# New ranks for the convolution and preparation stages, delta-A weights on GpSimd, and five projection chunks in flight, in a selective-scan and attention kernel on one core

## The chip, the core and the metric

The kernel runs on one NeuronCore of a Trainium2 chip. Five engines work there side by side, each through its own instructions in a fixed order: TensorE (PE in the profile; its weight loads are PEld), VectorE (DVE), ScalarE (ACT), GpSimd (POOL) and SyncE (SP), which here issues all transfers. They wait for each other through semaphores. The metric is the device time of one execution in microseconds (us). The kernel before took 10973.58 us in the median of three runs (10972.01 to 10994.84).

## The reference, cut to what matters

Eight images of 96 channels and 64 x 64 pixels go through two layers. L is 4096 pixels, DI is 192 inner channels, K is 4 scan directions with 16 states each.

```python
# layer 0: x = x + conv_block(group_norm(x))
xh = layernorm(xh)                         # over the 96 channels
xi, z = split(xh @ in_proj_w.T + in_proj_b)   # 192 + 192 channels
xi = silu(depthwise_conv3x3(xi) + conv_b)
xs = stack([xi by rows, xi by columns] and both reversed)   # 4 directions
dts, Bs, Cs = split(xs @ x_proj_w)
delta = softplus(dts @ dt_proj_w + dt_proj_b)
A = -exp(A_log)
h[t] = exp(delta[t] * A) * h[t-1] + delta[t] * xs[t] * B[t];  y[t] = C[t] . h[t]
y = sum of the 4 directions, put back in place, + D * xs
out = (layernorm(y) * silu(z)) @ out_proj_w.T + out_proj_b
# layer 1: t = t + linear attention(layernorm(t)); t = t + quantised MLP(layernorm(t))
```

## The kernel before, in words

The images are taken in four pairs. For each pair there is a **scan** (line 586 on), some 1910 us long, in which DVE runs one scan instruction after the other. Between two scans lie two planned stages. In the first, `back` (line 825) turns the last pair's scan output into the input of the second layer while `project` (line 369) normalises and projects the new pair's images, in 16 chunks of 512 pixels. In the second, `tail` (line 963) runs the MLP of the last pair, in 16 chunks, while `convolve` (line 457) and `prepare` (line 503) make the scan's inputs for the new pair. Pair 0 has no `back` or `tail` beside it; after the last scan there is only `back` and then `tail`. Before the first `convolve`, `decay_weights` (line 282) makes the weights from which TensorE forms delta times A: from `A_log` it makes three bf16 parts, sends them to DRAM in 24 small transfers, reads them back spread over the partitions (`ac`), multiplies them with a mask into four tiles `awp` of 128 x 6144 bf16 (line 317) and writes these to DRAM (line 322), from where the scans load them.

**The planner.** Within a planned stage every instruction is first put down in a list (`P.add`) with its engine, a cost, what it reads and writes, the ring of buffers that it takes a buffer from, and a rank. `P.run` then emits them one by one with a clock of its own. On each engine it takes, among the instructions that could start within 0.1 us of the earliest one, that with the smallest rank:

```python
least = min(f[0] for f in found)
choices.append(min((f for f in found if f[0] <= least + 0.1), key=lambda f: (f[1], f[2])))
```

On the chip each engine then keeps to that order. An ACT instruction can name a set of tables (`"ln"`, `"silu"`, `"softplus"`); a table load is needed whenever the set changes.

**project.** A chunk is scaled with the group statistics (DVE, L423), normalised over channels by `norm` (PE L357, ACT square, PE L361, ACT Ln and Exp, DVE L365), scaled (DVE L428), and goes through three matmuls (L432, L438, L444), which ACT evacuates into the padded images and, with Silu, into `zt`, which is stored. The ring `chunk` of three empty slots allows three chunks in flight; PSUM has three banks `q` and two `hold`; there are eight `small` tiles when `back` is not beside it, and six when it is.

**convolve.** The 192 channels of both images lie in three tiles. Tiles 0 and 2 are convolved on DVE: for each image half h, 9 instructions of 128 x 2048 a tile (L473 and L476), which makes 36 a pair. Tile 1 goes through TensorE: 9 matmuls (L483) a chunk of 512 pixels, 72 a pair. Then ACT applies Silu to every chunk of `xi`. The ranks are -2 for half 0 and -1 for half 1, ahead of all that `prepare` and `tail` do.

**prepare.** For two pixel orders o, 8 chunks c, two directions k and three tiles T there is a unit of work, 96 a pair: TensorE makes the projections (L543, shared by three units, and L555), ACT the softplus `d` and its first bf16 part, DVE `du` = d * u (L560) and the remainder `rest` (L571), ACT the second part, POOL the third (L576); then 384 KB of `dp` and 256 KB of `du` go to DRAM for the scan. The rings are short: three `d`, `du` and `dp`, two `rest`, four PSUM banks `big`, which the convolution's matmuls also take. For o = 0 a unit of chunk c needs only chunk c of `xi`; for o = 1 POOL first copies the pixels in column order (`u`, L535, 24 a pair), which needs all chunks. The rank is (8 o + c) / 16.

**tail.** Its chunk i had rank i / 16, three chunks in flight; its norm needs the `"ln"` tables, the units of `prepare` need `"softplus"`.

`xi` is allocated where the tiles of `decay_weights` lay: tile 0 of `xi` and half of tile 1 overlap `awp`, so the first write of either waits until the last `awp` has been written to DRAM.

Of the kernel before, what the change touches and what calls it, by code (L numbers as in the profile page):

```python
# [14 lines left out]
AF = mybir.ActivationFunctionType  # L15
ALU = mybir.AluOpType
# [3 lines left out]
DIM = 96  # L20
# [6 lines left out]
F = 512  # L27
# [129 lines left out]
def vss_attn_ffn(ctx: ExitStack, tc: tile.TileContext, a: dict):  # L157
    nc = tc.nc
# [31 lines left out]
    convb = load("convb", [128, 2])  # L190
# [91 lines left out]
    def decay_weights():  # L282

        with tc.tile_pool(name="aprep", bufs=1) as wp:
            am = wp.tile([128, KD, 2, NS], F32, name="am")
            nc.sync.dma_start(am, a["alog"])
            nc.scalar.activation(am, am, AF.Exp)  # L290
            nc.vector.tensor_scalar(am, am, -1.0, None, ALU.mult)
            for i in range(3):
                ap = wp.tile([128, KD, 2, NS], BF16, name=f"ap{i}")
                nc.vector.tensor_copy(ap, am)
                if i < 2:
                    nc.vector.tensor_tensor(am, am, ap, ALU.subtract)
                for k in range(KD):
                    nc.sync.dma_start(ad[i, k, 0:128], ap[:, k, 0])
                    nc.sync.dma_start(ad[i, k, 128:DI], ap[0:64, k, 1])
            mask = wp.tile([128, 16], F32, name="mask")  # L300
            for p in range(3):
                nc.sync.dma_start(
                    mask[32 * p : 32 * p + 32],
                    ident[0:16, 0:16].unsqueeze(1).to_broadcast([16, 2, 16]),
                )
            for p in range(2):
                nc.sync.dma_start(mask[96 + 16 * p : 112 + 16 * p], ident[0:16, 0:16])
            for k in range(KD):
                ac = wp.tile([128, NE * NS], BF16, name="ac", bufs=2)
                for i, rows, n in ((0, slice(0, 96, 2), 6), (1, slice(1, 96, 2), 6), (2, slice(96, 128), 4)):  # L310
                    nc.sync.dma_start(
                        ac[rows],
                        ad[i, k].rearrange("(s c) n -> s (c n)", s=8).unsqueeze(0)
                        .to_broadcast([n, 8, NE * NS]),
                    )
                aw = wp.tile([128, 48, 16, 8], BF16, name="awp", bufs=2)
                nc.vector.tensor_tensor(
                    aw,
                    ac.rearrange("p (c n) -> p c n", n=8).unsqueeze(2).to_broadcast([128, 48, 16, 8]),
                    mask.unsqueeze(1).unsqueeze(3).to_broadcast([128, 48, 16, 8]), ALU.mult,  # L320
                )
                nc.sync.dma_start(awd[k], aw.rearrange("p c m n -> p (c m n)"))
# [43 lines left out]
            dst(), P["ncp" + n][:DIM], P["nrs" + n], ALU.mult, **kw),  # L366
            ("ncp" + n, "nrs" + n), written, new, rank)

    def project(P, pair, zs, ybuf, p1):

        pad = [t.rearrange("p (h w) -> p h w", w=HH + 2) for t in ybuf]
        for T in range(3):
# [6 lines left out]
        dma(P, 0.03, lambda: swap[:, 64:128], lambda: a["winT"][:, 128:DI], (), ("swap#1",), rank=-1)  # L379
        ring(P, p1, "xt", 2, [DIM, L])  # L380
        ring(P, p1, "zt", 2, [128, 2, F])
        P.ring("chunk", [None] * 3)
        stat = [[p1.tile([DIM, w], F32, name=f"{n}{b}") for n, w in (
            ("mv", 2), ("gm", 1), ("gd", 1), ("gv", 1), ("gr", 1))] for b in range(2)]
        bst = [p1.tile([DIM, NCH, 6], F32, name=f"bst{b}") for b in range(2)]
# [71 lines left out]
    def convolve(P, xi, ybuf, p1):  # L457

        pad = [t.rearrange("p (h w) -> p h w", w=HH + 2) for t in ybuf]
        diag = p1.tile([128, 9, 128], F32, name="diag")  # L460
        for t in range(9):
            dve(P, 0.28, lambda t=t: nc.vector.tensor_scalar(
                diag[:, t, :], ident, convw[:, 0, t : t + 1], None, ALU.mult), (), (f"diag#{t}",), (), -2)
        for h in range(2):
            for T in (0, 2):
                for t in range(9):
                    dy, dx = divmod(t, 3)
                    w = convw[:, half(T), t : t + 1]
                    v = pad[T][:, 32 * h + dy : 32 * h + dy + HH // 2, dx : dx + HH]
                    o = xi[T].rearrange("p (h w) -> p h w", w=HH)[:, 32 * h : 32 * h + HH // 2]  # L470
                    wr = [f"xi{T}#{c}" for c in range(4 * h, 4 * h + 4)]
                    if t == 0:
                        dve(P, 1.4, lambda o=o, v=v, w=w: nc.vector.tensor_scalar(  # L473
                            o, v, w, None, ALU.mult), (), wr, (), -2 + h)
                    else:
                        dve(P, 2.34, lambda o=o, v=v, w=w: nc.vector.scalar_tensor_tensor(  # L476
                            o, v, w, o, ALU.mult, ALU.add), (), wr, (), -2 + h)
            for c in range(4 * h, 4 * h + 4):
                r0 = c * ROWS
                n = f"pc.{c}"  # L480
                for t in range(9):
                    dy, dx = divmod(t, 3)
                    mm(P, 0.87, lambda n=n, t=t, r0=r0, dy=dy, dx=dx: nc.tensor.matmul(  # L483
                        P[n], diag[:, t, :], pad[1][:, r0 + dy : r0 + dy + ROWS, dx : dx + HH],
                        start=(t == 0), stop=(t == 8)), (f"diag#{t}",), (n,), ((n, "big"),), -2 + h)
                act(P, lambda c=c: xi[1][:, bass.ts(c, F)], lambda n=n: P[n], AF.Identity, 0.68, (n,),
                    (f"xi1#{c}",), (), -2 + h, bias=convb[:, 0:1])
        for c in range(NCH):
            for T in range(3):
                b_ = 0.0 if T == 1 else convb[:, half(T) : half(T) + 1]  # L490
                act(P, lambda T=T, c=c: xi[T][:, bass.ts(c, F)], lambda T=T, c=c: xi[T][:, bass.ts(c, F)],
                    AF.Silu, 0.72, (), (f"xi{T}#{c}",), (), -1 + c / 10, "silu", bias=b_)

    def spread(P, size, dst, T, src, reads, writes, rank):

# [467 lines left out]
    def tail(P, pair, t1, tn, tmp):  # L963
# [11 lines left out]
        for i in range(2 * NCH):  # L975
            c, b = divmod(i, 2)
            cs = bass.ts(c, F)
            rank = i / 16
            n = f"t.{i}"
            tf, xa, pa, t2, tq, hq, p2, y16, ot = (  # L980
                v + n for v in ("tf", "xa", "pa", "t2", "tq", "hq", "p2", "y16", "ot"))
# [42 lines left out]
    for pair in range(npair + 1):  # L1024

        new = {}
        if pair < npair:
            for name, shape, dtype in (
                ("zs", [2, DI, L], F32), ("us", [2 * DI, L], F32),
                ("dl", [KD, NT * TC // WC, 3, 16, NE, WC], BF16), ("du", [KD, NT, 16, NE, TC], F32),  # L1030
                ("bs", [KD, NT // NB, 2 * NS, NB * TC], F32),
                ("cs", [KD, NT // NB, 2 * NS, NB * TC], F32), ("ys", [KD, 16, L, NE], F32),
                ("t1", [2, DIM, L], F32), ("tn", [2, DIM, L], F32),
            ):
                new[name] = dram.tile(shape, dtype, name=name)
        with ExitStack() as pads, ExitStack() as xis:
            if new:

                yp = pads.enter_context(tc.tile_pool(name="yp", bufs=1, side="right"))
                ybuf = [yp.tile([128, (HH + 2) ** 2], F32, name=f"y{T}") for T in range(3)]  # L1040
            with ExitStack() as st:
                st.enter_context(tc.manual_schedule())
                P = Plan()
                tmp = st.enter_context(tc.tile_pool(name="bk", bufs=1))
                psum = banks(P, st, q=3, hold=2, **({"py": 2} if old else {}))
                ring(P, tmp, "small", 6 if old else 8, [DIM, F])
                if old:
                    back(P, pair - 1, old["ys"], old["us"], old["zs"], old["t1"], old["tn"], tmp, psum)
                if new:
                    project(P, pair, new["zs"], ybuf,  # L1050
                            st.enter_context(tc.tile_pool(name="p1", bufs=1, side="right")))
                P.run(table)
            if pair == 0:
                decay_weights()
            if new:
                xp = xis.enter_context(tc.tile_pool(name="xip", bufs=1))
                xi = [xp.tile([128, L], F32, name=f"xi{T}") for T in range(3)]
            with ExitStack() as st:
                st.enter_context(tc.manual_schedule())
                P = Plan()  # L1060
                tmp = st.enter_context(tc.tile_pool(name="tt", bufs=1))
                banks(P, st, **({"q": 3, "hold": 1} if old else {}), **({"big": 4} if new else {}))
                if old:
                    ring(P, tmp, "small", 4, [DIM, F])
                    tail(P, pair - 1, old["t1"], old["tn"], tmp)
                if new:
                    convolve(P, xi, ybuf, tmp)
                    prepare(P, tmp, xi, new["us"], new["dl"], new["du"], new["bs"], new["cs"])
                P.run(table)
        if new:  # L1070
            scan(new["dl"], new["du"], new["bs"], new["cs"], new["ys"])
        old = new
# [114 lines left out]
```

## Time and profile before

| | |
|---|---|
| median of three runs | 10973.58 us (10972.01 to 10994.84) |
| the profiled execution's own time | 10968.08 us |
| its span, from the first to the last instruction | 10966.3 us, granted TensorE clock 0.836 |
| busy: PE, DVE, ACT, POOL | 7884.5, 9068.7, 6970.9, 8003.3 us |
| first `project`, alone | 34 to 185 us |
| `decay_weights` after it | to 229 us |
| `convolve` and `prepare` of pair 0 | 229 to 613 us |
| the other three second stages (`tail`, `convolve`, `prepare`) | 2841 to 3316, 5538 to 6008, 8225 to 8699 us |
| the last `tail`, alone | 10853 to 10966 us |

Engine rows give busy time within a stretch and, in brackets, how many instructions ran. A row of instructions gives line, engine, operation, output and inputs, shape; a bracket at its end tells how long the engine had been idle and what ended that. L332 is the helper `act`, L351 the helper `dma`, L357 to L365 `norm`.

### The profile page before, as it was taken

To read this page: it belongs to the slowest core of one execution; us is meant where nothing else is said; L and a number is where in the kernel's file an instruction comes from. 1 tells how busy PE (TensorE), PEld (TensorE's weight loads), DVE (VectorE), ACT (ScalarE), POOL (GpSimd) and SP (SyncE) were. 2 spreads that over 40 slices of the span, in tenths; PEclk is the share of its full clock that TensorE was granted. 3 is DMA by queue.
4 is the path that set the end of the run, shared out by engine and by line. 5 is a ranking of instruction groups with operands and counts; after the bars stand their busy time and mean duration, and the time that the engine had idled before them with its cause. 6 is when DMAs were issued, how large, how long until landed. Compare 5 with 4: busy or idle time off the path is not lost. (4 is left out here: it accounts for less than half of the span.)

```text
span 10966.3 us, 379334 instructions
## 1 busy us (share of the span) xinstructions
PE 7884.5 (72%) x163328; PEld 5514.9 (50%) x163328; DVE 9068.7 (83%) x6702; ACT 6970.9 (64%) x12201; POOL 8003.3 (73%) x2802
## 2 busy tenths in 40 slices
PE   6756666668985666666987666666698666666678
PEld 2245555555424555555532555555553255555554
DVE  4689999996668999999566999999857699999975
ACT  3566666665566666666556666666665566666654
POOL 0579999993148999999124999999813599999961
PEclk8678888889877888888987888888897788888889
DMA  2777777779477777777847777777785777777775
GB/s 78 207 200 197 205 202 198 203 201 208 124 193 202 202 201 201 202 202 201 201 132 200 197 200 203 202 201 205 190 184 161 195 199 201 203 203 203 201 194 143
DMA packets 1761606, 2095.80 MB, mean 191 GB/s; under 512 B 440371, under 2 KB 1343028, under 8 KB 1756340
## 3 DMA queue, kind: packets, MB, share of 16 engines
q1 hardware_dynamic: 1759924, 2071.52, 71.9%
q8 instruction: 1282, 21.00, 0.9%
q14 instruction: 400, 3.28, 0.1%
HBM read 1606.82 MB, written 464.01 MB: 189 GB/s over the span
## 5 line engine op out<-in xcount | busy, mean ns | idle before, releaser
L743 DVE TENSOR_TENSOR_SCAN h<-da,dbu 128x774 f32<-128x774 f32 x4096 | 7026.2, 1759 | 561.2 <-POOL dbu L707 340.6
L707 POOL TENSOR_TENSOR dbu<-dut,bc 128x1536 f32<-128x1536 f32 x2048 | 7092.2, 3505 | 484.7 <-DMA dut<-du 157.4
L732 ACT ACTIVATE da<-da 128x768 f32<-128x768 f32 x4092 | 3246.5, 796 | 2417.2 <-PE da L725 2386.4
L725 PE MATMUL da<-dm,aw 128*128 128x128 bf16 x24576 | 2508.7, 249 | 2565.9 <-DVE h L743 1835.8
L725 PEld LDWEIGHTS <-aw 128*128 128x128 bf16 x24576 | 1883.7, 110 | 2886.3 <-issue 2012.6
L761 PE MATMUL yp<-h,cw 128*32 128x48 f32 x131072 | 2965.9, 244 | 29.7 <-issue 16.2
L761 PEld LDWEIGHTS yp<-h,cw 128*32 128x32 f32 x131072 | 2456.2, 155 | 511.4 <-issue 240.0
L661 ACT ACTIVATE cw<-bc,blk 128x512 f32<-128x512 f32 x2048 | 1469.8, 719 | 93.8 <-DMA bc<-cs 90.5
L576 POOL TENSOR_TENSOR dp<-rest,dp 128x512 bf16<-128x512 f32 x384 | 456.4, 1192 | 659.5 <-ACT dp L332 600.8
L866 POOL TENSOR_TENSOR yd<-yk 128x768 f32<-128x768 f32 x64 | 124.7, 1948 | 780.0 <-DMA yk<-ys 366.7
L555 PE MATMUL big<-S,dtw 12*128 12x512 f32 x768 | 513.7, 796 | 112.9 <-ACT d L332 89.8
L535 POOL COPY u<-xi 128x512 f32<-128x512 f32 x96 | 205.9, 2161 | 526.9 <-ACT xi L332 495.8
L769 ACT ACTIVATE yev<-yp 128x384 f32<-128x384 f32 x1024 | 504.7, 493 | 42.3 <-PE yp L761 41.6
L571 DVE TENSOR_TENSOR rest<-d,dp 128x512 f32<-128x512 f32 x384 | 348.5, 913 | 201.2 <-ACT dp L332 161.3
L332 ACT ACTIVATE dp<-rest 128x512 bf16<-128x512 f32 x384 | 239.3, 628 | 300.3 <-DVE rest L571 299.0
L704 ACT COPY dbu<-h 128x12 f32<-128x12 f32 x1984 | 410.8, 207 | 0.0
L555 PEld LDWEIGHTS big<-S,dtw 12*128 12x128 f32 x768 | 155.6, 228 | 431.8 <-ACT d L332 221.2
L332 ACT ACTIVATE small<-hold 96x512 f32<-96x512 f32 x192 | 113.7, 592 | 318.3 <-PE hold L357 303.4
L560 DVE TENSOR_TENSOR du<-d,u 128x512 f32<-128x512 f32 x192 | 208.3, 1091 | 118.1 <-ACT d L332 118.1
L880 PEld LDWEIGHTS py<-ident,yd 128*96 128x96 f32 x2048 | 245.2, 165 | 91.7 <-issue 82.6
L476 DVE SCALAR_TENSOR_TENSOR xi<-y,c_convw,xi 128x2048 f32<-128x2048 f32 x128 | 290.3, 2347 | 0.0
L880 PE MATMUL py<-ident,yd 128*96 128x128 f32 x2048 | 262.0, 275 | 13.9 <-DVE yd L866 9.2
(122 smaller groups left out, 6009.0 us busy)
## 6 DMA issues: line engine op xcount, KB each, us to landing
dut<-du SPq DMA_DIRECT2D x2048, 384.0 KB
dm<-dl SPq DMA_DIRECT2D x2048, 144.0 KB
dl<-dp SPq DMA_DIRECT2D x256, 384.0 KB
dm<-dl SPq DMA_DIRECT2D x2048, 48.0 KB
ys<-yev SPq DMA_DIRECT2D x1024, 96.0 KB
du<-du SPq DMA_DIRECT2D x256, 256.0 KB
bc<-cs SPq DMA_DIRECT2D x512, 128.0 KB
bc<-bs SPq DMA_DIRECT2D x512, 128.0 KB
```

Source lines behind the costliest of these rows:

```text
L332: "ACT", cost, lambda: nc.scalar.activation(dst(), src_(), func, **kw),
L555: mm(P, 1.0, lambda pq=pq, k=k, T=T, S=S: nc.tensor.matmul(P[pq], dtw[64:76, k, T], P[S][64:76], start=True, stop=True), (S, "dtw"), (pq,) ...
L576: P.add("POOL", 1.24, lambda rest=rest, dp=dp, w=w: nc.gpsimd.tensor_tensor(P[dp][:, :, 2], w(rest), P[dp][:, :, 1], ALU.subtract), (rest, ...
L661: nc.scalar.activation(cw[i % 2][:, :, :, m, :].rearrange("p z j t -> p (z j) t"), bc[i][:, 1].rearrange("p z (j t) -> p (z j) t", j=NB), ...
L704: nc.scalar.copy(start, segs(hs[s - 1][:, :, r])[:, :, :, 1 if back else TC])
L707: nc.gpsimd.tensor_tensor(segs(t)[:, :, :, 1:], dut[g].unsqueeze(1) .to_broadcast([128, 2, NI, TC]), bc[s // NB][:, 0, :, bass.ts(c % NB, ...
L725: nc.tensor.matmul(e[:, i], aw[k, r][:, i, z, :], dm[s // 2][:, NI * r + i, bass.ts(c % 2, TC)], start=True, stop=True,)
L732: nc.scalar.activation(e, e, AF.Exp)
L743: nc.vector.tensor_tensor_scan(hs[s][:, w, r][:, d], da[p % 3][:, o : o + W6][:, d], dbu[4 * s + r][:, w][:, d], 0.0, ALU.mult, ALU.add,)
L761: nc.tensor.matmul(y[32 * q : 32 * q + 32, 2 * NE * i : 2 * NE * i + 2 * NE] .rearrange("p (j r i) -> p i j r", j=2, r=NR), w[:, z, :, t], ...
L769: nc.scalar.activation(yev[s][:, :, o : o + 8, :].rearrange("p j i e -> p i j e"), y[:, 0 : 16 * NE].rearrange("p (i j e) -> p i j e", j=2 ...
L880: nc.tensor.matmul(o, P[yd][:, k, j, DIM * g : DIM * g + DIM], ident, start=(k + j == 0), stop=(k + j == 4),)
```

## The change

Four edits. (1) `convolve`: half 0 keeps rank -2; half 1, on DVE, PE and ACT, gets rank 0.2 and so stands after the o = 0 units of chunks 0 to 3 where both could start; so do the Silus of chunks 4 to 7. (2) `tail`: the rank goes from i / 16 to 0.25 + 0.75 i / 16. (3) `project` without `back` beside it, that is for pair 0 alone: five chunks in flight instead of three, four banks `q` and four `hold` instead of three and two, ten `small` tiles instead of eight. (4) `decay_weights`: the six small instructions on `am` and the four multiplications into `awp` move from DVE to GpSimd.

```diff
@@ decay_weights
-            nc.vector.tensor_scalar(am, am, -1.0, None, ALU.mult)
+            nc.gpsimd.tensor_scalar(am, am, -1.0, None, ALU.mult)
...
-                nc.vector.tensor_copy(ap, am)
+                nc.gpsimd.tensor_copy(ap, am)
                 if i < 2:
-                    nc.vector.tensor_tensor(am, am, ap, ALU.subtract)
+                    nc.gpsimd.tensor_tensor(am, am, ap, ALU.subtract)
...
-                nc.vector.tensor_tensor(
+                nc.gpsimd.tensor_tensor(
                     aw,
                     ac.rearrange("p (c n) -> p c n", n=8).unsqueeze(2).to_broadcast([128, 48, 16, 8]),
                     mask.unsqueeze(1).unsqueeze(3).to_broadcast([128, 48, 16, 8]), ALU.mult,
@@ project
-    def project(P, pair, zs, ybuf, p1):
+    def project(P, pair, zs, ybuf, p1, beside):
...
-        P.ring("chunk", [None] * 3)
+        P.ring("chunk", [None] * (3 if beside else 5))
@@ convolve
         for h in range(2):
+            first = 0.2 if h else -2
...
-                            o, v, w, None, ALU.mult), (), wr, (), -2 + h)
+                            o, v, w, None, ALU.mult), (), wr, (), first)
...
-                            o, v, w, o, ALU.mult, ALU.add), (), wr, (), -2 + h)
+                            o, v, w, o, ALU.mult, ALU.add), (), wr, (), first)
...
-                        start=(t == 0), stop=(t == 8)), (f"diag#{t}",), (n,), ((n, "big"),), -2 + h)
+                        start=(t == 0), stop=(t == 8)), (f"diag#{t}",), (n,), ((n, "big"),), first)
...
-                    (f"xi1#{c}",), (), -2 + h, bias=convb[:, 0:1])
+                    (f"xi1#{c}",), (), first, bias=convb[:, 0:1])
...
-                    AF.Silu, 0.72, (), (f"xi{T}#{c}",), (), -1 + c / 10, "silu", bias=b_)
+                    AF.Silu, 0.72, (), (f"xi{T}#{c}",), (), -1 + c / 10 if c < 4 else 0.2, "silu", bias=b_)
@@ tail
-            rank = i / 16
+            rank = 0.25 + 0.75 * i / 16
@@ the loop over the pairs
-                psum = banks(P, st, q=3, hold=2, **({"py": 2} if old else {}))
-                ring(P, tmp, "small", 6 if old else 8, [DIM, F])
+                psum = banks(P, st, **({"q": 3, "hold": 2, "py": 2} if old else {"q": 4, "hold": 4}))
+                ring(P, tmp, "small", 6 if old else 10, [DIM, F])
...
                     project(P, pair, new["zs"], ybuf,
-                            st.enter_context(tc.tile_pool(name="p1", bufs=1, side="right")))
+                            st.enter_context(tc.tile_pool(name="p1", bufs=1, side="right")), bool(old))
```

## The prediction

> **What bounds the kernel now.** I first set the order of instructions of both programs side by side. The four scans, the three stages of `back` with `project`, and the last `back` and `tail` are the same, instruction for instruction. Only 34 to 613 us and the three second stages can change. I read their busy times by stretch (stretch, length, then PE, PEld, DVE, ACT, POOL, granted TensorE clock, DMA share, GB/s).
>
> ```profile
> 34.00:184.00 150.00, 99.36 (x168) 34.83 (x168) 37.94 (x78) 89.79 (x131) 0.00 (x0) 0.82 0.21 57
> 228.90:306.10 77.20, 53.48 (x104) 20.60 (x104) 77.19 (x36) 23.06 (x37) 31.29 (x1) 0.79 0.18 60
> 306.10:466.00 159.90, 131.77 (x200) 36.55 (x200) 94.79 (x106) 99.83 (x174) 70.88 (x58) 0.71 0.91 235
> 466.00:613.00 147.00, 104.68 (x153) 27.83 (x152) 93.75 (x93) 83.71 (x145) 78.75 (x63) 0.66 0.82 211
> 2841.00:2922.00 81.00, 79.56 (x174) 33.59 (x173) 80.66 (x50) 22.04 (x34) 14.58 (x4) 0.92 0.24 79
> 2922.00:3184.00 262.00, 220.50 (x401) 70.01 (x400) 160.88 (x250) 184.07 (x308) 90.95 (x76) 0.74 0.66 177
> 3184.00:3316.00 132.00, 96.21 (x150) 28.18 (x148) 85.46 (x92) 80.11 (x141) 73.82 (x60) 0.69 0.89 228
> 10853.00:10966.00 113.00, 77.34 (x192) 27.21 (x192) 60.36 (x146) 62.00 (x112) 19.53 (x19) 0.88 0.27 84
> ```
>
> DVE is full while it convolves (rows 2 and 5). Nothing is full in the rest. Preparation alone takes 132 us for its last 44 units (row 7), 3.0 us each, and 3.0 us in pair 0 too (28 units from 373 to 457 us). At that pace 96 units are 288 us; the stretch 2922 to 3316 is 394 us, so the 16 chunks of `tail` cost 106 us, 6.6 each, hardly less than alone (110 us, row 8). The stage therefore adds up: 81 + 288 + 106 = 475 us. Two streams that share it save next to nothing by sharing.
>
> The DVE timeline shows what starts the convolution of pair 0, and the pace of the first `project`:
>
> ```profile
> 121.28 1.28 DVE L365 TENSOR_TENSOR xt<-hold,small 96x512 f32<-96x512 f32 x2 [14.02 <-ACT small L332]
> 138.37 1.28 DVE L365 TENSOR_TENSOR xt<-hold,small 96x512 f32<-96x512 f32 x2 [13.99 <-ACT small L332]
> ...
> 197.39 26.29 DVE L317 TENSOR_TENSOR awp<-ac,mask 128x6144 bf16<-128x6144 bf16 x4 [19.67 <-DMA ac<-ad]
> 228.91 2.48 DVE L473 TENSOR_SCALAR xi<-y,c_convw 128x2048 f32<-128x2048 f32 x2 [5.24 <-DMA awd<-awp]
> 231.31 36.28 DVE L476 SCALAR_TENSOR_TENSOR xi<-y,c_convw,xi 128x2048 f32<-128x2048 f32 x16
> ```
>
> Two chunks go through `project` in lockstep every 17.1 us, and DVE idles 14 of them behind ACT. The convolution waits for the store of `awp`, over which `xi` lies, so the multiplications are on the path whichever engine runs them.
>
> The rows of POOL by line (count, then min/median/max in ns) give the prices there:
>
> ```profile
> L866 POOL TENSOR_TENSOR yd<-yk x64: 1798/1814/3228, 2560.6 to 10799.4; 128x768 f32<-128x768 f32 x64
> L707 POOL TENSOR_TENSOR dbu<-dut,bc x2048: 3415/3504/3683, 633.4 to 10598.6; 128x1536 f32<-128x1536 f32 x187
> L576 POOL TENSOR_TENSOR dp<-rest,dp x384: 1142/1154/1672, 313.0 to 8697.7; 128x512 bf16<-128x512 f32 x192
> L535 POOL COPY u<-xi x96: 1047/1507/35298, 274.8 to 8654.7; 128x512 f32<-128x512 f32 x96
> ```
>
> The 35.3 us in the last row is one copy that began at 274.8, five microseconds into the 36.28 us run of L476, and ended at 310.1, after that run and the five short DVE instructions behind it (309.2).
>
> [...] a POOL copy got no turn between back-to-back DVE instructions. [...] L576 shows 1154/512 = 2.25, L866 2.36. [...]
>
> **The change, part by part.**
>
> *Project of pair 0.* Before, the last round's load of the Ln and Exp tables stands at 169.4 us, six rounds of 17.1 after that at 66.5, and the stage ends at 185.2. In the new order three rounds of four chunks stand between a first and a last of two; the table loads fall from 16 to 10. A four-chunk round on ACT: four squares at 0.59, four Ln and Exp at 0.6 each, eight pads and eight Silus at 0.62, 17.1 us, plus two loads, 2.6: 19.7. Bubbles: after the Exps come 0.7 + 0.5 us on DVE and matmuls that at first end 1.7 us apart (the pads at 176.4, 178.1 and 180.0 us show it), which holds ACT up by about 3 us, and the last squares wait some 2: 24.5 us for four, against 34.2. First load 4 us earlier (a fourth bank), one round of 26, two of 24.5: the last round's load stands at 62.5 + 26 + 24.5 + 24.5 = 137.5 instead of 169.4. That is **-32 us**, between -20 (rounds of 28) and -38. ACT's `am` exponential keeps its place in that last round, so all behind it moves along.
>
> *Delta-A weights.* The small instructions add 0.5 us before the first of the 24 transfers, which take 15.8 us of SP's issue as before. Then 4 x 6144 x 2.25 ns = 55.3 us on POOL in place of 26.3 on DVE: +29. L866, with inner runs of 24 elements, pays 0.11 ns an element more; the runs here are of 8, three times as many, so 0.33 more: 63.4 us, +37. No row shows such runs. I take **+33**, from +28 to +55 (about three times that surcharge). DVE idles meanwhile[...] and gains nothing, as it waits for `xi`. So edits 3 and 4 cancel: the convolution starts at about 228 us again.
>
> *Ranks, conv and prepare.* In the new order of DVE 18 instructions of half 0 and 5 of half 1 come first, then 20 units with the other 13 between them, then the rest. The first part takes 23 x 2.26 = 52 us. In the second POOL must run 20 x 1.15 us; DVE 40 short ones at 0.60 (issue to issue) and 13 at 2.26: 24 + 29.4. [...] if streams add as before it is 20 x 3.0 + 29.4 = 89.4. `rest` has two buffers, so after two units DVE stops for POOL, [...] I take 81. Before, 36 instructions and 20 units took 81 + 60 = 141; now 52 + 81 = 133. That is **-8 us** a stage, from -13 to +10; pair 0 the same with -9, as its first units ran slower (21 in 67 us).
> Costs inside it: six more table loads a stage (24 for 18; pair 0: 10 for 4, paid by `project`), 7.7 us[...]; uncovered they leave nothing. Half 1's matmuls now share `big` with the units; [...] SP: a `dp` store issued in turn waits for a POOL part that is late, and the `tf` and `xa` loads of `tail` queue behind it; `tail` starts later by rank, so this is not first.
>
> *Ranks, tail.* Its 16 chunks now end 18 units before the stage's end, not 41. As the streams add, where they meet costs nothing: 0, from -15 (sharing at last) to +10.
>
> Sum for the profiled execution: -32 + 33 - 9 - 3 x 8 = -32 us, 10968.1 to 10936; the median of the runs lies 5.5 above that execution, so **10942 us**. What a measurement can tell from no change is about 0.2%, 22 us.
>
> **Rivals.**
> *Cancelled* (0.26): the ranks give nothing, since streams add (89.4, hence 0), and edits 3 and 4 balance: 10974, -22 to +22. For it: the sum rule above. Against it: the 13 gaps are filled by work that needs only DVE.
> *Stores start early* (0.12): preparation is bound by its stores (DMA share 0.91, 235 GB/s in row 3), so starting them half a convolution, 38.6 us, earlier ends each of four stages that much earlier: 10974 + 1 - 154 = 10821. Against it: 3.0 us a unit also at share 0.82, and 0.66 in the mixed stretch.
> *POOL starved* (0.18), slower: [...] `rest` and `dp` are not freed, and units wait in turn. At 100 us for that part each of four stages is 19 longer than forecast: 10942 + 76 = 11018. It decides from 81 + (32 + 22)/4 = 95 us on.
>
> **From numbers to chances.** The forecast's case, a saving of 22 to 60 us (10913 to 10951), has 0.44. With *stores start early* faster has 0.56; same 0.26; slower 0.18. The range leaves out most of the early stores and about half of the starved case, and spans the rest: 10868 to 11015.
>
> **What would show it.** `project` of pair 0 ends near 152 us, L317 on POOL at about 14 us each, L473 starts at 222 to 236; DVE without a gap from there until the 36th convolution, some 135 us later; each later second stage 455 to 475 us. A POOL L576 of over 5 us, or the 36th convolution later than 150 us, means starvation. The forecast falls if L317 takes 20 us or if `tail` and units begin to overlap.

## The result and the profile after

The changed kernel takes 10958.63 us in the median of 17 runs (10932.0 to 10978.22), the kernel before 10974.37 us on the same chip (17 runs, 10960.55 to 11002.45): a ratio of 0.9981, with a 95% interval of 0.9974 to 0.9989, or 16 us less, half of what was forecast. So little is the rest of some larger changes. From the two profiled executions (spans 10966.3 and 10960.2 us), cut at the same instructions:

| stretch | before | after | difference | forecast |
|---|---|---|---|---|
| start to the last matmul of the first `project` | 183.8 | 147.5 | -36 | -32 |
| exponential of `am` to the first convolution instruction | 53.2 | 75.8 | +23 | +33 |
| pair 0, first convolution instruction to last `rest` | 382.5 | 374.2 | -8 | -9 |
| the same, pair 1 | 471.2 | 472.3 | +1 | -8 |
| the same, pair 2 | 464.6 | 470.8 | +6 | -8 |
| the same, pair 3 | 468.6 | 472.7 | +4 | -8 |

The first and the third step came out near the forecast, the second ten under it. The three second stages did not: they were to give 24 us and took 11. The rows sum to -10 us, and the two spans differ by 6, because stretches whose instructions are the same in both differ too: from the last `rest` of pair 2 to the convolution of pair 3 it is 21 us more in the second execution, behind the last `rest` of pair 3 14 us less. Busy times of the engines by stretch in the changed kernel (stretch, length, PE, PEld, DVE, ACT, POOL, granted TensorE clock, DMA share, GB/s): the first `project`; pair 0 to the 36th convolution instruction; then the second stage of pair 1 in three parts, to the 23rd convolution instruction, to the 21st `rest`, and to the last `rest`.

```profile
34.00:147.50 113.50, 88.38 (x168) 33.05 (x168) 36.74 (x72) 77.99 (x122) 2.26 (x6) 0.89 0.27 76
216.00:338.50 122.50, 83.44 (x143) 26.95 (x143) 116.89 (x75) 61.87 (x98) 39.85 (x20) 0.73 0.52 141
2818.50:2866.30 47.80, 47.80 (x109) 20.21 (x109) 47.80 (x24) 12.76 (x20) 0.00 (x0) 0.97 0.29 89
2866.30:2950.80 84.50, 71.45 (x124) 22.53 (x123) 74.63 (x60) 57.38 (x90) 43.42 (x22) 0.78 0.71 187
2950.80:3290.80 340.00, 279.74 (x488) 87.30 (x486) 204.55 (x296) 224.54 (x379) 140.53 (x113) 0.72 0.69 183
```

The DVE timeline of the changed kernel, where the first `project` ends, shows that the wait for the store of `awp` is still the last one before the convolution:

```profile
137.04 1.28 DVE L365 TENSOR_TENSOR xt<-hold,small 96x512 f32<-96x512 f32 x2 [18.53 <-ACT small L332]
...
216.01 2.48 DVE L474 TENSOR_SCALAR xi<-y,c_convw 128x2048 f32<-128x2048 f32 x2 [76.77 <-DMA awd<-awp]
```

And this is what it waits for on POOL (timeline), two multiplications of 10.5 us, a gap for `ac`, and two more:

```profile
162.02 21.00 POOL L317 TENSOR_TENSOR awp<-ac,mask 128x6144 bf16<-128x6144 bf16 x2 [18.82 <-DMA ac<-ad]
189.50 21.00 POOL L317 TENSOR_TENSOR awp<-ac,mask 128x6144 bf16<-128x6144 bf16 x2 [6.48 <-DMA ac<-ad]
```

The gap is new: before, the four ran without one (the line of L317 in the prediction). In SP's timeline five of the six transfers of the last two `ac` stand behind the store of the second `awp`, and so behind the second multiplication:

```profile
172.56 0.34 SPq L322 DMA_DIRECT2D awd<-awp  x1
173.09 0.72 SPq L311 DMA_DIRECT2D ac<-ad  x1
183.04 0.33 SPq L322 DMA_DIRECT2D awd<-awp  x1
183.42 4.79 SPq L311 DMA_DIRECT2D ac<-ad  x5
```

POOL's rows by line (count, then min/median/max in ns) say that nothing there starved. The longest copy takes 3.1 us, not 35.3, for no copy now waits behind more than one convolution instruction; the maximum of L577 doubles to 3.2 us, about what it takes when one convolution instruction (2.35 us) stands ahead of it:

```profile
L577 POOL TENSOR_TENSOR dp<-rest,dp x384: 1142/1156/3202, 267.6 to 8705.7; 128x512 bf16<-128x512 f32 x192
L536 POOL COPY u<-xi x96: 1032/1508/3132, 313.7 to 8661.5; 128x512 f32<-128x512 f32 x96
```

### The profile page after: what moved, and what is told of

Its sections match the earlier page's. It is cut to its first block, busy times and chain, and to the rows that moved or that the text cites. A ratio compares the mean times of both kernels' runs of the same rounds, so it can differ in the third digit from the quotient of the medians.

```text
span 10960.2 us, 379332 instructions
## 1 busy us (share of the span) xinstructions
PE 7869.0 (72%) x163328; PEld 5499.1 (50%) x163328; DVE 9050.0 (83%) x6692; ACT 6997.2 (64%) x12219; POOL 8055.0 (73%) x2812
## 5 line engine op out<-in xcount | busy, mean ns | idle before, releaser
L762 PEld LDWEIGHTS yp<-h,cw 128*32 128x32 f32 x131072 | 2449.4, 155 | 515.1 <-issue 239.0
L577 POOL TENSOR_TENSOR dp<-rest,dp 128x512 bf16<-128x512 f32 x384 | 522.6, 1365 | 896.6 <-ACT dp L332 880.7
L477 DVE SCALAR_TENSOR_TENSOR xi<-y,c_convw,xi 128x2048 f32<-128x2048 f32 x128 | 315.2, 2508 | 0.0
L484 PE MATMUL big<-y,diag 128*128 128x512 f32 x576 | 278.1, 629 | 40.9 <-ACT xi L332 32.8
```

Of the source, the lines that this page charges most:

```text
L577: P.add("POOL", 1.24, lambda rest=rest, dp=dp, w=w: nc.gpsimd.tensor_tensor(P[dp][:, :, 2], w(rest), P[dp][:, :, 1], ALU.subtract), (rest, ...
L762: nc.tensor.matmul(y[32 * q : 32 * q + 32, 2 * NE * i : 2 * NE * i + 2 * NE] .rearrange("p (j r i) -> p i j r", j=2, r=NR), w[:, z, :, t], ...
```

## The experiments

Every ratio is against runs of the kernel before in the same session, as its median lay between 10958.7 and 11028.7 us from one session to another.

**Each edit by itself.** Theory at this point: the edits add up, and the later `tail` is what costs the second stages their gain. The rival: the ranks of the convolution cost it themselves. Each of these four is the kernel before with one edit.

*e1_project*: edit (3) alone.

```diff
-        P.ring("chunk", [None] * 3)
+        P.ring("chunk", [None] * (3 if beside else 5))
...
-                ring(P, tmp, "small", 6 if old else 8, [DIM, F])
+                ring(P, tmp, "small", 6 if old else 10, [DIM, F])
```

> The kernel before with the edits to the first project alone (five chunks, q 4, hold 4, ten small). Theory (edits add up): the last matmul of project at 147 to 149 us instead of 183.8 (-36), the exponential of am at about 140 instead of 175.6, the first instruction of the convolution at 228.9 - 36 = 193 us (the multiplications stay on DVE), and the whole kernel -36 us, ratio 0.9967. Rival (what project saves is given back behind it, since stores of zs then pile up ahead of delta-A's transfers): convolution not before 205 us and a ratio of 0.998 or more.

Measured: last matmul at 150.0, the convolution starts at 195.8 us, 33 earlier than before; ratio 0.9976 (0.9966 to 0.9986), which is 15 to 37 us. The saving passes on to the convolution whole.

*e2_decay*: edit (4) alone, the ten instructions of `decay_weights` on GpSimd.

```diff
-                nc.vector.tensor_tensor(
+                nc.gpsimd.tensor_tensor(
                     aw,
```

> The kernel before with delta-A's instructions on GpSimd alone. Theory: L317 takes 10.5 us each on POOL as in the changed kernel, the time from the exponential of am to the first instruction of the convolution grows from 53.3 to 76 us, nothing else moves: +22.6 us, ratio 1.0021. Rival (DVE, freed, gains something elsewhere): the convolution starts as late, but the ratio stays under 1.001.

Measured: L317 takes 10.52 us, the convolution starts at 253.2 instead of 228.9 us; ratio 1.0026 (1.0015 to 1.0036). It is a plain loss of some 24 us: DVE has nothing to do in the time that it is given.

*e3_conv_ranks*: edit (1) alone, with `tail` at i / 16; the cut shows one of the lines that take the new rank.

```diff
+            first = 0.2 if h else -2
...
-                            o, v, w, o, ALU.mult, ALU.add), (), wr, (), -2 + h)
+                            o, v, w, o, ALU.mult, ALU.add), (), wr, (), first)
```

> The kernel before with the ranks of convolution and Silu alone; tail keeps rank i/16. Theory (the later tail costs what the second stages lost): pair 0 gains 8 us from the start of its convolution to its last rest, the three second stages (first convolution instruction to last rest: 471.2, 464.6 and 468.7 before) gain 8 each as forecast: 460 on the mean, total -33 us, ratio 0.997. Rival (the ranks of the convolution cost it themselves, by six more table loads a stage and a mixed stretch that takes longer): second stages at 470 to 473 as in the changed kernel, total within 5 us of before, ratio 0.9995 to 1.0005.

Measured: pair 0 -8.5 us, and the second stages 443.7, 443.3 and 443.3 us: **-25 each**, three times what the theory said; ratio 0.993 (0.9915 to 0.9944). Both expectations missed it, and both had the price of the convolution's ranks wrong. Which of the lines of edit (1) do it (DVE, PE, ACT, the Silus) was not separated.

*e4_tail_rank*: edit (2) alone.

```diff
-            rank = i / 16
+            rank = 0.25 + 0.75 * i / 16
```

> The kernel before with the later rank of tail alone. Theory (the later tail costs): pair 0 as before, second stages about 12 us longer each (480 on the mean), total +36 us, ratio 1.003; the last 16 chunks take 7.2 us each beside the units, instead of 6.6. Rival (streams add up, where they meet costs nothing): 468 on the mean, ratio 1.000.

Measured: 481.2, 479.0 and 481.5 us, +12 each as the theory said, and pair 0 as before (382.9); ratio 1.002 (1.0013 to 1.0027), which is 14 to 30 us where the stages alone sum to 37.

So edits (1) and (2) do not add. The later `tail` costs 12 us a stage by itself, and 471.9 - 443.4 = 28.5 us once the convolution's second half is spread. Where that happens shows in the busy times of DVE. The second stage of pair 1 in three parts, as in the fence above; only in the kernel before, where all 36 convolution instructions come first, the first cut is behind the 36th. The kernel before:

```profile
2844.70:2921.90 77.20, 77.20 (x170) 32.41 (x170) 77.20 (x38) 22.04 (x34) 12.95 (x1) 0.94 0.23 74
2921.90:3024.40 102.50, 85.71 (x155) 26.65 (x154) 63.46 (x95) 75.35 (x122) 37.39 (x31) 0.75 0.70 191
3024.40:3315.90 291.50, 231.10 (x396) 71.64 (x394) 182.96 (x247) 188.74 (x325) 127.48 (x104) 0.72 0.75 195
```

The kernel with the convolution's ranks alone:

```profile
2844.80:2898.00 53.20, 53.20 (x122) 21.71 (x120) 50.35 (x29) 18.43 (x27) 0.00 (x0) 0.97 0.34 107
2898.00:2991.00 93.00, 82.57 (x157) 28.16 (x156) 81.21 (x91) 63.17 (x106) 62.48 (x24) 0.78 0.67 176
2991.00:3288.60 297.60, 245.50 (x443) 76.19 (x441) 188.62 (x260) 203.62 (x349) 134.78 (x111) 0.76 0.77 202
```

DVE's busy time is nearly one and the same, 324 us before, 320 here, 327 in the changed kernel. What differs is how long it idles. Before: nothing, 39.0 and 108.5 us in the three parts. Convolution's ranks alone: 2.9, 11.8 and 109.0. Changed kernel: nothing, 9.9 and 135.4. The first edit fills 24 us of DVE's waits ahead of the third part, and the later `tail` opens 26 us of them again in the third. As the busy time is the same, this says where a stage gets longer, not why.

Counting `tail`'s DVE instructions (nine a chunk) gives the chunks in each part. To the 21st `rest` the changed kernel runs 0.3 chunks and takes 132.3 us, the one with the convolution's ranks alone 4.1 chunks in 146.2 us: 13.9 / 3.8 = 3.7 us a chunk, no more than the 3.8 us that a chunk keeps DVE busy in the last `tail` (60.36 us for 16). Behind it, with 75 units at 3.0 us (225 us) taken off, a chunk costs (297.6 - 225) / 11.9 = 6.1 us there, and (340.0 - 225) / 15.7 = 7.3 us in the changed kernel.

The 3.0 us are low, though. Pair 0 runs the same 75 units with no `tail` beside them; in the changed kernel:

```profile
344.98:590.22 245.24, 193.96 (x301) 55.27 (x299) 146.41 (x153) 148.60 (x257) 119.67 (x97) 0.70 0.86 223
```

That is 3.3 us a unit (244.9 us for the 75 with the convolution's ranks alone). With pair 0's times of the same execution taken off, a chunk costs 4.2 us ahead of the 21st `rest` and 4.4 us behind it with the convolution's ranks alone, and 6.0 us behind it in the changed kernel. So it is not shown that a place beside the convolution is what makes a chunk cheap.

What pair 0 does give is the price of the whole `tail`, a second stage (mean of the three) less pair 0's: 86 us before, 98 with the later `tail` alone, 69 with the convolution's ranks alone, and 98 with both. With the later `tail`, edit (1) is worth 9 us a stage, as much as in pair 0. With `tail` at i / 16 it is worth 16 us more, and those lie in the price of `tail`.

The DVE timeline with the convolution's ranks alone shows a chunk (L365, L988, L998) between units and convolution, with no idle time in brackets on any row:

```profile
2917.29 0.68 DVE L365 TENSOR_TENSOR tq<-hold,small 96x512 fp8e5<-96x512 f32 x1
...
2918.86 0.67 DVE L988 TENSOR_TENSOR t<-xa,q 96x512 f32<-96x512 f32 x1
2919.46 2.34 DVE L477 SCALAR_TENSOR_TENSOR xi<-y,c_convw,xi 128x2048 f32<-128x2048 f32 x1
...
2923.30 0.60 DVE L998 TENSOR_SCALAR h<-h,b1q 128x512 f16<-128x512 f16 x2
...
2924.75 2.34 DVE L477 SCALAR_TENSOR_TENSOR xi<-y,c_convw,xi 128x2048 f32<-128x2048 f32 x1
```

**Undoing the one edit.** *k5_after_old_tail* is the changed kernel with `rank = i / 16` in `tail`.

```diff
-            rank = 0.25 + 0.75 * i / 16
+            rank = i / 16
```

> The changed kernel with tail's rank set back to i/16, all other edits kept. Theory (the convolution's second half fills DVE's waits only if tail is there to share it; the later tail takes that away): second stages 443 us each as with the conv ranks alone, instead of 472; convolution of pair 0 still at 216 us; against before -36 + 22.6 - 8 - 3 x 25 = -97 us, ratio 0.991. Rival (the gain of the conv ranks alone depended on something else of that kernel): second stages of 460 or more, ratio over 0.995.

Measured: stages of 443.5, 450.6 and 443.6 us, the convolution of pair 0 at 218.2 us; ratio 0.9913 (0.9888 to 0.9937). One line of the change had cost about 75 us (0.9981 - 0.9913), 78 by the stages. Single stages of some 450 instead of 443 us turn up in other runs with these ranks too. PE's order in the third part is the same in both kinds, but the granted clock is lower in the longer one, and the part is longer by about as much as PE's busy time. The third parts of pairs 1 and 2 in k5:

```profile
2970.35:3267.82 297.47, 245.48 (x443) 76.29 (x441) 188.71 (x260) 203.72 (x349) 134.97 (x111) 0.76 0.77 202
5649.92:5954.12 304.20, 253.39 (x444) 78.37 (x442) 186.14 (x261) 204.54 (x349) 134.70 (x111) 0.74 0.75 198
```

**More of the same.** *k7_project_conv* keeps only edits (1) and (3): delta-A stays on DVE, `tail` at i / 16. *k8_tail_early* is k7 with `rank = i / 32`.

> The kernel before with two of the four edits: the first project's buffers and the ranks of convolution and Silu; delta-A on DVE, tail at i/16. Theory (edits add): convolution of pair 0 at 196 us, second stages 443 us: -34 - 8 - 75 = -117 us, ratio 0.9893. Rival: less than -100 us, ratio over 0.991.

> The kernel of k7 with tail's rank at i/32, so that more of its chunks run while DVE has instructions of the convolution to fill with. Theory (a chunk beside the convolution costs only its 3.8 us of DVE, a later one 6 to 7): some four more chunks move there, second stages 430 to 440 us instead of 443: 0.9860 to 0.9893 against before. Rival (the units then come late and their stores pile up at the end): second stages of 450 us or more.

Measured for k7: the convolution of pair 0 at 193.9 us, stages of 449.6, 443.2 and 450.7 us, ratio 0.9889 (0.9866 to 0.9911), as the sum of the edits says. For k8: stages of 458.7, 464.1 and 458.4 us, ratio 0.9926 (0.9898 to 0.9953): the number of the rival; its reason, stores that pile up, was not traced. The 6.3 chunks in the first two parts do cost little (153.4 us, 3.5 a chunk by the first sum above), but 9.7 more follow quickly, the last ends 291 us into the stage, and in the third part a chunk costs (305.3 - 225) / 9.7 = 8.3 us, or 6.3 with pair 0's 244.4 us taken off. Of the three ranks of `tail` tried with the convolution's new ones, the early and the late one are both worse than the even one.

Why `tail` costs 69 us in one order and 98 in another was not settled. In all five orders PE is busy for 79 to 83% of the third part and DVE for 60 to 63%; in the changed kernel the part also has 15 table loads on ACT instead of 10. In pair 1 the granted clock of the third part goes roughly with the price of a chunk there (over pair 0's units): 0.76 and 4.4 us with the convolution's ranks alone, 0.72 and 5.2 before, 0.72 and 6.0 in the changed kernel, 0.71 and 6.3 in k8, 0.70 and 6.4 with the later `tail` alone. Whether the clock is a cause of the price or only goes with the order, no run tells, as none changed PE's work or the table loads alone.

**Can GpSimd hide delta-A?** *k6_right* is k5 with the tiles of `decay_weights` elsewhere, so that `xi` doesn't lie over them.

```diff
-        with tc.tile_pool(name="aprep", bufs=1) as wp:
+        with tc.tile_pool(name="aprep", bufs=1, side="right") as wp:
```

> The kernel of k5 with the buffers of delta-A (am, ap, ac, awp) on the other side of SBUF, so that xi no longer lies over awp and the convolution doesn't wait for its last store. Theory (GpSimd can hide delta-A only when nobody waits for its buffer): the convolution starts at 150 to 160 us instead of 216; [...] last rest of pair 0 comes 20 to 60 us earlier than in k5 (590): at 530 to 570, ratio against before 0.986 to 0.989. Rival ([...] DVE waits for each multiplication, or POOL gets its turn only after the 23 first convolution instructions and the units wait behind it): last rest within 15 us of k5, ratio 0.990 to 0.992.

Measured: the convolution starts at 140.9 instead of 218.2 us, but the last `rest` of pair 0 comes at 581.7, only 11 us earlier than in k5 (592.6); ratio 0.9905 (0.9879 to 0.9931). The rival is right, and the timelines of k6 show both halves of it. On POOL, a multiplication of 128x128 that takes 0.53 us in the changed kernel:

```profile
159.40 29.71 POOL L291 TENSOR_SCALAR am<-am 128x128 f32<-128x128 f32 x1 [156.69 <-DMA mask<-ident]
```

It ended at 189.1 us. On DVE, the end of the run behind which it stood, at 188.7 us (two instructions in it, L474, have one tile as input), and then DVE's own wait for the four late L317:

```profile
179.46 2.48 DVE L474 TENSOR_SCALAR xi<-y,c_convw 128x2048 f32<-128x2048 f32 x2
181.85 6.87 DVE L477 SCALAR_TENSOR_TENSOR xi<-y,c_convw,xi 128x2048 f32<-128x2048 f32 x3
...
256.74 1.62 DVE L572 TENSOR_TENSOR rest<-d,dp 128x512 f32<-128x512 f32 x1 [49.40 <-POOL dp L577]
```

*k10_early_decay* is k7 with `decay_weights` ahead of the first `project`, on GpSimd and GpSimd's queue, in a pool that stays open until `project` is done; *k11_pieces* cuts each of its multiplications into eight.

```diff
+    early = ExitStack()
+    decay_weights(early.enter_context(tc.tile_pool(name="aprep", bufs=1)))
...
-            if pair == 0:
-                decay_weights()
+            if pair == 0:
+                early.close()
```

```diff
+                for j in range(0, 48, 6):
+                    nc.gpsimd.tensor_tensor(
+                        aw[:, j : j + 6],
```

> The kernel of k7 (first project, ranks of convolution and Silu; tail at i/16) with delta-A made at the very start, on GpSimd and with its transfers on GpSimd's queue, in a buffer of its own below those of project. Theory (delta-A costs only since the convolution waits for its buffer; GpSimd and its queue have nothing during project): the four multiplications end before 130 us, the convolution of pair 0 starts when project ends, at 150 to 156 us instead of 194: about -40 us on k7, ratio against before 0.985 to 0.987. Rival (GpSimd's reads hold up DVE and with it ACT in project, or the transfers on its queue are slow): project ends 10 us or more later, ratio 0.987 to 0.989.

> The kernel of k10 with each multiplication on GpSimd cut into eight of 768 elements. In k10 a DVE instruction of 96x1 with two inputs stood 9.2 us behind an L317, and project ended at 168.2 us instead of 148. Theory [...]: no DVE instruction of project waits over 2.5 us, project ends at 150 to 153, the convolution starts by 145, last rest of pair 0 at 530 to 536 instead of 549.7, ratio against before 0.985 to 0.987. Rival [...]: DVE waits for the end of a run of sixteen, 20 us in place of 9, project ends at 168 or later, and the time is that of k10, 0.9875, or more.

Measured for k10: the last multiplication ends at 112 us, but `project` ends at 168.2 us, 20 later than in k7; the convolution starts at 159.6 and the last `rest` of pair 0 comes at 549.7 (k7: 563.4); ratio 0.9875 (0.9859 to 0.9892): the rival. For k11: `project` ends at 159.6, the convolution starts at 151.4, last `rest` at 540.8; 10847.72 us against 10999.39 before, ratio 0.9868 (0.9851 to 0.9886). That is the lowest ratio here and beats both kernels; its interval and those of k6, k7 and k10 overlap. The theory was half right. In k10 (DVE timeline) an instruction of 96x1 stands behind one L317:

```profile
70.88 9.22 DVE L404 TENSOR_TENSOR gd<-mv,gm 96x1 f32<-96x1 f32 x1
```

In k11 the same instruction, now L406, gets through after one piece, while L430 waits for seven, twice (the second line holds two instructions, of 0.53 and 10.70 us):

```profile
66.32 1.19 DVE L406 TENSOR_TENSOR gd<-mv,gm 96x1 f32<-96x1 f32 x1
...
72.89 10.04 DVE L430 TENSOR_SCALAR xt<-xt,c_nw,c_nb 96x512 f32<-96x512 f32 x1
...
104.20 11.15 DVE L430 TENSOR_SCALAR xt<-xt,c_nw,c_nb 96x512 f32<-96x512 f32 x2
```

The pieces on POOL in k11 that the first of them waited for:

```profile
72.57 10.07 POOL L318 TENSOR_TENSOR awp<-ac,mask 128x768 bf16<-128x768 bf16 x7
```

**Two prices.** *e8_prices* adds five instructions to the changed kernel, in the code behind the last L317 (two of them ran ahead of the four L317):

```diff
+            nc.gpsimd.tensor_tensor(fo, fb, fa, ALU.mult)
+            nc.gpsimd.tensor_tensor(
+                f4(fo), f4(fb),
+                mask.unsqueeze(1).unsqueeze(3).to_broadcast([128, 48, 16, 8]), ALU.mult,
+            )
+            nc.gpsimd.tensor_tensor(
+                f4(fo), ac.rearrange("p (c n) -> p c n", n=8).unsqueeze(2).to_broadcast([128, 48, 16, 8]),
+                f4(fa), ALU.mult,
+            )
+            nc.gpsimd.tensor_tensor(fo[:, 0:512], fa[:, 0:512], fb[:, 0:512], ALU.subtract)
+            nc.gpsimd.tensor_tensor(fa[:, 0:1536], fa[:, 1536:3072], fa[:, 3072:4608], ALU.mult)
```

> The changed kernel with five more instructions on GpSimd behind the fourth L317, while DVE has nothing: (a) the multiplication of 6144 elements, bf16 times f32 to bf16, without any broadcast; (b) with the mask's broadcast only; (c) with ac's only; (d) the form of L576, 512 elements, f32 minus bf16 to bf16; (e) the form of L707, 1536 elements, all f32, but plain rows. L317 took 10.52 us, 1.71 ns an element, where the rows of before said 2.25. Theory A (a broadcast operand is cheaper to read): (a) 13.8 us, (b) or (c) about 10.5, (d) 1.15 and (e) 3.5 us as in the rows of before. Theory B ([...] GpSimd alone takes 1.71 ns): (a), (b) and (c) 10.5 us, (d) 0.88, (e) 2.63 us. Theory C (the number of bytes decides): (a) to (d) at 1.71 to 1.8 ns an element, (e) at 2.25.

POOL's timeline of this kernel:

```profile
152.64 11.87 POOL L329 TENSOR_TENSOR fo<-fb,fa 128x6144 bf16<-128x6144 bf16 x1 [8.93 <-DVE fb L327]
164.58 10.74 POOL L330 TENSOR_TENSOR fo<-fb,mask 128x6144 bf16<-128x6144 bf16 x1
...
223.72 10.55 POOL L334 TENSOR_TENSOR fo<-ac,fa 128x6144 bf16<-128x6144 bf16 x1
234.34 1.15 POOL L338 TENSOR_TENSOR fo<-fa,fb 128x512 bf16<-128x512 f32 x1
235.57 3.42 POOL L339 TENSOR_TENSOR fa<-fa 128x1536 f32<-128x1536 f32 x1
```

Plain rows take 1.93 ns an element, either broadcast some 10% less (1.75 and 1.72), both together no less (1.71). DVE had nothing from 152.6 to 239.0 us. The short forms take what they take in the rows of before (1.15 us, the median there, and 3.42, the shortest there), here with DVE idle: theory B falls, C falls too (1.93 and 2.25 ns for what it put at 1.71 to 1.8), and A holds in direction, though it doesn't explain 1.93 against 2.25. The two differ in the operation, the place of the bf16 operand and the length; which of them counts is open.

*e9_port* is the kernel before with a memset of 128x8 on DVE behind each two-input instruction of the convolution.

```diff
+                    dve(P, 0.0, lambda: nc.vector.memset(gap, 0.0), (f"xi{T}#{4 * h}",), ("gap",), (), -2 + h)
```

> The kernel before with one memset of 128x8 on DVE behind each of the 32 two-input instructions of the convolution, nothing else. Theory [...]: the copy of pair 0 that took 35.3 us, from five microseconds into that run to its end, takes under 6 us now, and the convolution gets longer by that turn and by 32 x 0.06 = 2 us. Rival (POOL is let in only when DVE has nothing to issue): the copy takes over 30 us again.

Measured: the first two copies of pair 0 together take 4.12 us. The first had to wait for nobody: its input, a Silu, was ready at 277.91 us, and a memset of 0.07 us ended at 277.95. The second began while a convolution instruction ran and got in behind the next memset. The convolution instructions behind the two memsets take 3.21 and 3.03 us instead of 2.35. The timelines of POOL and DVE:

```profile
277.97 4.12 POOL L537 COPY u<-xi 128x512 f32<-128x512 f32 x2 [275.26 <-DVE gap L479]
```

```profile
277.97 3.21 DVE L477 SCALAR_TENSOR_TENSOR xi<-y,c_convw,xi 128x2048 f32<-128x2048 f32 x1
281.13 0.07 DVE L479 MEMSET gap<- 128x8 f32 x1
281.21 3.03 DVE L477 SCALAR_TENSOR_TENSOR xi<-y,c_convw,xi 128x2048 f32<-128x2048 f32 x1
```

That is a turn of under 6 us, as the theory forecast, seen at one place of one execution. But POOL got a turn without a memset too. In the changed kernel, which has none, the second of these two L577 got its turn between two convolution instructions: it began at 316.72, the first L477 ended at 318.90, the L577 at 319.91, and the second L477 took 3.12 us.

```profile
315.15 4.76 POOL L577 TENSOR_TENSOR dp<-rest,dp 128x512 bf16<-128x512 f32 x2
```

```profile
315.67 6.39 DVE L477 SCALAR_TENSOR_TENSOR xi<-y,c_convw,xi 128x2048 f32<-128x2048 f32 x2
```

The planner mixes the last convolution instructions with units in e9, so its time (11013.48 against 11003.99 us, one run) isn't that of the memsets alone.

## Why the prediction was right and where it was wrong

**Direction right, size half.** 10942 us was forecast and 10958.6 measured: within the range (10868 to 11015), but outside the likeliest case's own (10913 to 10951), and with 0.19% just under what the text called measurable (17 runs do tell it from nothing). That it fell into the range is in part luck: `project` gave 4 us more and delta-A cost 10 less than forecast, which hid some of the 35 us that the second stages came out worse.

**Project: right.** -36 for -32. The table loads did fall from 16 to 10, counted from the start of the program. Each takes 1283 ns in both traces, with the next instruction some 20 ns behind it (before: load at 169.42 us, Ln at 170.72); the trace of before has 152 of them, one at the start and one at each of the 151 changes of the set. And the rounds lost less time than the bubbles that were allowed for.

**Delta-A: right that it is on the path whichever engine runs it, too dear by ten.** +23 for +33. Two terms were off, against each other. The multiplications cost 16 us more than on DVE (42.0 us for 26.3), not 29 to 37: they took 1.71 ns an element where the sum had 2.25 and a surcharge for short inner runs, the author's estimate from L866; a broadcast operand made them cheaper, not dearer (e8: 10.74 and 10.55 us for 11.87). And the wait of 6.5 us for `ac` stood in no term.

**Ranks, conv and prepare: near by luck in pair 0, and with one share left out.** To the 21st `rest` the changed kernel took 132.3 us in pair 1 against a forecast of 133; the first part was shorter than its sum (47.9 us for 52, as four of the 23 instructions are of 1.2 us and not 2.26), the second longer (84.5 us for 81, which was the author's estimate). POOL did not starve (from the 23rd to the 36th convolution instruction it took 76 us, far from the 95 at which that rival decides). Pair 0 gained 8.3 us for a forecast of 9, but as -15.4 up to the 21st `rest` and +7.1 behind it, where the forecast had nothing. And the sum charged every chunk of `tail` 6.6 us wherever it runs. With the convolution's ranks alone the whole `tail` costs 16 us less than before, and the edit is worth -25 us a stage, not -8. The 6.6 itself rests on 3.0 us a unit, the pace of the last 44; pair 0 took 305 us for its 96 units, which leaves (394 - 305) / 16 = 5.6 us a chunk. (Alone, by row 8, the 16 chunks take 113 us, not 110.)

**Ranks, tail: the step that failed.** "As the streams add, where they meet costs nothing: 0, from -15 (sharing at last) to +10." Where they meet cost 28.5 us a stage: 12 that the later `tail` costs by itself, and 16 that the convolution's ranks would have saved in `tail`. The rule was fitted to a profile in which the convolution lay ahead of everything, and was then used for an order in which it doesn't. The two edits were costed one after the other, each against the kernel before, when the second takes away most of what the first gives. The six more table loads a stage, 7.7 us at 1283 ns each, were put with the convolution's ranks and taken as hidden, which was the author's estimate: but with the convolution's ranks alone there are 18 a stage, as before, and with both edits 24, so they belong to the two together. How much of the 28.5 us is theirs no run tells.

**The rivals.** *Cancelled* forecast 10974 +- 22 and holds the result, but its reason is wrong: the ranks did give something, and it was the other edit of them that took it back. *Stores start early* is refuted: in pair 0 the first store of `dp` was issued 53 us behind the first convolution instruction instead of 85, and it still gained only 8 us. *POOL starved* did not come about in the changed kernel, though POOL can stand behind a run of convolution instructions on DVE: in k6 it did, for 29.7 us.

## What to carry to other kernels

When two streams share the engines, the price of one depends on the order (69 to 98 us for the same `tail` here), so cost edits to an order together: the second can take away what the first gives. Take the price of a stream from a stretch where it runs alone from end to end, as pair 0 did, and not from the pace of its last part. In this kernel it paid to spread the convolution's second half among the units and `tail` evenly over the stage, neither early nor late. Before moving work to an idle engine, see who waits for its buffer and which engine may have to wait beside it: GpSimd was slower on the path (42.0 us for DVE's 26.3), and off the path it stood behind DVE (29.7 us in k6) or DVE behind it (9.2 us in k10, 10.0 and 10.7 in k11).

## What the runs showed of the hardware

- A GpSimd instruction that began during a run of convolution instructions on DVE could last until that run was over: 35.3 us for a copy in the kernel before, which ended 4 us behind the run, and in k6 29.71 us for an instruction of 128x128 (0.53 us in the changed kernel), which ended 0.4 us behind the run. In k6 the run held two TENSOR_SCALARs, and GpSimd's instruction lasted past both. In e9, with a DVE memset of 0.07 us between convolution instructions, two copies took 4.12 us together; in the changed kernel GpSimd once got its turn between two convolution instructions without a memset (two L577 in 4.76 us). What decides when GpSimd gets its turn was not found.
- DVE stood behind GpSimd too. In k10 an instruction of 96x1 with two inputs took 9.22 us beside multiplications of 10.5 us, and 0.14 us for the other image, with none beside it. In k11, with pieces of about 1.45 us, it took 1.19 us, while a TENSOR_SCALAR with one tile as input (L430, 0.54 us with none beside it) twice lasted until seven back-to-back pieces were over (10.04 and 10.70 us). Two other pairs of L430 beside pieces took 2.19 and 3.21 us a pair; what decides was not found.
- A GpSimd multiplication of 6144 elements, f32 and bf16 to bf16, took 11.87 us with plain rows (e8) and 10.5 to 10.7 us with a broadcast operand (e8 and the changed kernel).
